# A four-layer gated cross-attention and experts block: layer 0's expert weights kept, attention in parts of TensorE's array, layer 3 as one pipeline

## The chip, the core and the metric

The kernel runs on one core of a Trainium2 chip. Five engines of the core work side by side, each with its own list of instructions in order: TensorE (PE: matmuls, transposes, and loads of its stationary operand, shown as PEld), VectorE (DVE), ScalarE (ACT), GpSimd (POOL) and SyncE (SP, which here only starts DMA transfers). They meet through semaphores. Matmul results land in PSUM, everything else lives in SBUF (128 partitions) or in device memory.

The metric is the device time of one execution in microseconds, the median of several runs. Everything is float32; in the profile one such matmul appears as two instructions, one transpose as one.

## The reference

`x` is 2 × 1024 tokens of width 256, the context 2 × 64 tokens. Four layers follow each other; each adds a gated attention on the context and then a gated feed-forward part, both on a normalised `x`:

```python
x = x + tanh(g_xattn[l]) * attention_l(layernorm(x), ctx)
x = x + tanh(g_ffn[l]) * ffn_l(layernorm(x))
```

What differs is the kind. With 16 heads of width 16 (layers 1 and 3):

```python
score = einsum('bhqd,bhkd->bhqk', qh, kh) / sqrt(16)
score = where(mask, score, -large)      # L1: a key mask; L3: a mask per query and key
out = einsum('bhqk,bhkd->bhqd', softmax(score), vh) @ Wo + bo
```

| layer | attention | feed-forward |
|---|---|---|
| 0 | linear, elu + 1 | each token to 1 of 8 experts (256 to 1024 to 256, relu), no capacity |
| 1 | 16 heads, softmax over 64 keys | sum of 8 dense experts, silu gate |
| 2 | one head | 1 of 8 experts, at most 384 tokens each, gelu |
| 3 | 16 heads, masked per query | 2 of 8 experts, at most 320 tokens each, relu, weights normalised over the two |

## The kernel before

The 2048 tokens are 16 tiles of 128, four tiles to a group of 512. The residual stream `xs` stays in SBUF as [128, 16, 256]. A scheduler may move instructions within each engine's list, so the order in the program is a starting point, not the final list.

**Layer 0's experts** (`moe0`, L973). The tokens are routed (a softmax over 8 logits, the largest), ranked within their expert by matmuls with triangular matrices, and sorted by expert into 23 tiles of at most 128 tokens (2048/128 + 8 − 1, so that any distribution fits). How many tiles an expert has is known on the chip only, so the loop over tiles is fixed and reads everything through indices: `rows_of` (L1031) is an indirect DMA with one row index for each partition. Per tile GpSimd issues six: two of 1 MB for the weights (`w`, L1032), two for the biases (`b1j`, `b2j`), one that gathers 128 normalised token rows (`xg`, in `gather_T`, L861), and a scatter that adds the result into the residual in device memory (`xd`, in `ffn`, L899). `ffn` (L879) multiplies with the first weight (`mm256`, L217: 8 blocks of output × 2 halves of the contraction), adds the bias and activates on ScalarE (L887), multiplies with the second weight (L892), and adds bias and token weight on VectorE (L897, L898). The weights rotate through the six buffers of `wpool`.

**Attention with 16 heads** (`Heads`, L343). Per group, `queries` (L419) forms qᵀ. Per tile, `scores` (L430) multiplies two blocks of 128 query rows (8 heads) with a block-diagonal matrix `kblk` of the keys, 512 columns each; VectorE adds a key bias (L1) or writes −large by a mask (L3, L446), takes the row maxima (L460) and subtracts them (L461); ScalarE takes one exponential of 1024 columns (L464). `values` (L467) transposes the probabilities in eight blocks, copies them to SBUF (L150), and multiplies each block, as the stationary operand, with `vaug`: 34 columns of values and ones, so that a sum for each head comes along (L486). VectorE takes 16 reciprocals per token (L494) and scales (L496). `output` (L499) transposes the result (L504), copies it, multiplies by `Wo`, and adds to the residual on VectorE (L512); GpSimd adds the output bias (L513). `group` (L515) staggers four tiles: scores of tile i, values of i − 1, output of i − 2.

In layer 1 the first group runs alone and the second likewise early; the others run among the dense experts (`middle`, L1323, whose products are L1210 and L1255 and keep TensorE occupied). In layer 3 `heads_xattn` (L529) first normalises all four groups (`normed`, L209) and then takes the groups in turn.

**Layers 2 and 3's experts** (`moe_capacity`, L1053). All tokens are normalised, `route` (L740) chooses for all 16 tiles at once and ranks them with 16 stages of matmul (L788, L790), `invert` (L803) turns the slots into a list of tokens per expert by comparing with a ramp (L818 to L829) and one matmul per tile (L831). Then for each of 8 experts the weights are loaded by SP, three gathers are issued by GpSimd, and `gather_T` and `ffn` follow. The next use of `xs` waits for `reload` (L855). After layer 2's experts, `heads3.setup` and layer 3's attention follow, then layer 3's routing and experts, then the copy to the output.

Of the kernel before, what the change touches and what calls it, by code (L numbers as in the profile page):

```python
# [8 lines left out]
F32 = mybir.dt.float32  # L9
# [25 lines left out]
L0_NTILE = N // L0_W + E - 1  # L35
L2_CAP = 384
# [5 lines left out]
def kernel(ctx: ExitStack, tc: tile.TileContext, a: dict, out: bass.AP):  # L42
# [37 lines left out]

    spare = int_ramp([P, 1], [[0, 1]], N, 1, "spare")
# [21 lines left out]
    halfmask = group_mask(SK, 2, "halfmask")  # L103
    sel16 = const.tile([P, HD], F32, name="sel16")
# [238 lines left out]
    class Heads:  # L343


        def __init__(self, pre, c_bk, r_bv, r_bo, gate, key_mask, full_mask):
# [3 lines left out]
            self.live = {}  # L350

        def setup(self, psp, tag):
# [10 lines left out]
            vaug = self.vaug = held.tile([P, B, H // 2, 2, HD + 1], F32, name="vaug")  # L363
# [37 lines left out]
            for b in range(B):  # L401
# [5 lines left out]
                    vaug[:, b, :, :, 0:HD],  # L407
# [3 lines left out]
                V.tensor_copy(  # L411
                    vaug[:, b, :, :, HD],
                    halfmask.unsqueeze(1).to_broadcast([P, H // 2, 2]),
                )
            self.tg = gates[:, self.gate : self.gate + 1]
            self.bo = held.tile([P, D], F32, name="bo")
            V.tensor_scalar_mul(self.bo, rows[:, self.r_bo, :], self.tg)

        def queries(self, g, hT, pools):  # L419
            two, py = pools["two"], pools["py"]  # L420
            qT = two.tile([P, NC, GW], F32, name="qT", bufs=1)
# [6 lines left out]
            self.qT = qT  # L428

        def scores(self, tt, pools):  # L430
# [3 lines left out]
            pr = two.tile([P, H, SK], F32, name="pr")  # L434
            HC = H // NC
            for c in range(NC):
                ps = pss.tile([P, 512], F32, name="ps_s")
                T.matmul(  # L438
                    ps,
                    lhsT=self.qT[:, c, t * P : (t + 1) * P],  # L440
                    rhs=self.kblk[:, b, c].rearrange("p j k -> p (j k)"),
                    start=True, stop=True,
                )
                ps3 = ps.rearrange("p (j k) -> p j k", k=SK)
# [6 lines left out]
                prc = pr[:, c * HC : (c + 1) * HC, :]  # L451
                if self.key_mask is not None:
                    V.tensor_add(
                        prc, ps3,
# [3 lines left out]
                    ps3 = prc  # L458
                mx = two.tile([P, HC], F32, name="mx")
                V.tensor_reduce(mx, ps3, AX.X, ALU.max)  # L460
                V.tensor_tensor(  # L461
                    prc, ps3, mx.unsqueeze(2).to_broadcast([P, HC, SK]), ALU.subtract
                )
            A.activation(pr, pr, AF.Exp)  # L464
            self.live[tt] = pr

        def values(self, tt, pools):  # L467

# [15 lines left out]
            w = 2 * (HD + 1)  # L484
# [14 lines left out]
        def output(self, tt, pools):  # L499
# [3 lines left out]
            for c in range(NC):  # L503
                T.transpose(  # L504
                    pst[:, c * P : (c + 1) * P], of[:, c * P : (c + 1) * P], ident
                )
# [992 lines left out]
```

## Time and profile before

| | us |
|---|---|
| three runs | 2445.48, 2451.8, 2453.09 |
| their median | 2451.8 |
| the profiled execution, its own time | 2437.11 |
| its span in the trace | 2435.4 |

The profiled execution is somewhat shorter than the three runs. Its mean granted TensorE clock was 0.929 of full speed. The page shows where the work lies; this is its first part, the busy time of each engine, its share of the span and the instructions, and three rows of its second part, in which the span is cut into 40 slices of 61 us and each digit is tenths of a slice:

```profile
PE 2189.6 (90%) x10132; PEld 1782.7 (73%) x10132; DVE 1210.5 (50%) x2695; ACT 797.9 (33%) x1523; POOL 1054.2 (43%) x1189
...
PE   5668887899999999999999999999968996886997
...
PEclk9759998999999999999999999999958998895998
DMA  3138886012222122222122222222323443010442
```

Slices 4 to 7 are layer 0's experts (the DMA row is highest there); the long run of nines is the dense experts of layer 1 with layer 2's attention; the last third of the row has layer 2's experts, layer 3's attention, its routing (a low digit of the clock), and its experts. A high busy digit at a low clock digit is no full engine: the same work takes longer there.

### The profile page before, as it was taken

To read this page: it belongs to the slowest core of one execution; us is meant where nothing else is said; L and a number is where in the kernel's file an instruction comes from. 1 tells how busy PE (TensorE), PEld (TensorE's weight loads), DVE (VectorE), ACT (ScalarE), POOL (GpSimd) and SP (SyncE) were. 2 spreads that over 40 slices of the span, in tenths; PEclk is the share of its full clock that TensorE was granted. 3 is DMA by queue.
4 is the path that set the end of the run, shared out by engine and by line. 5 is a ranking of instruction groups with operands and counts; after the bars stand their busy time and mean duration, and the time that the engine had idled before them with its cause. 6 is when DMAs were issued, how large, how long until landed. Compare 5 with 4: busy or idle time off the path is not lost.

```text
span 2435.4 us, 27851 instructions
## 1 busy us (share of the span) xinstructions
PE 2189.6 (90%) x10132; PEld 1782.7 (73%) x10132; DVE 1210.5 (50%) x2695; ACT 797.9 (33%) x1523; POOL 1054.2 (43%) x1189
## 2 busy tenths in 40 slices
PE   5668887899999999999999999999968996886997
PEld 3457776588888778887788887888856774565775
DVE  5631113675565766655855656566551116663111
ACT  5313331343333533334433334333311222230221
POOL 4116664136666346665366664666402320000331
PEclk9759998999999999999999999999958998895998
DMA  3138886012222122222122222222323443010442
GB/s 98 43 110 245 249 257 223 0 55 88 92 86 88 44 70 87 87 87 74 55 91 91 87 89 77 89 87 87 130 79 86 130 122 95 18 51 30 117 117 51
DMA packets 97545, 235.08 MB, mean 97 GB/s; under 512 B 13184, under 2 KB 41088, under 8 KB 86976
## 3 DMA queue, kind: packets, MB, share of 16 engines
q1 hardware_dynamic: 70880, 159.14, 20.3%
q0 software_dynamic: 21456, 68.92, 10.3%
q10 hardware_dynamic: 5072, 5.23, 0.6%
q8 instruction: 81, 1.33, 0.2%
q14 instruction: 56, 0.46, 0.1%
HBM read 211.10 MB, written 24.25 MB: 97 GB/s over the span
## 4 chain that ended last, share of the span: by engine, by line
PE 76%; DVE 10%; DMA 4%; POOL 2%; ACT 2%; issue 2%; POOLq 0%; DVEq 0%; ACTq 0%; SPq 0%
PE ps_b L1210 13%; PE ps_m L217 11%; PE ps_e L1210 9%; PE ps_a L1210 9%; PE ps_y L892 8%; PE ps_b L1255 6%; PE ps_a L1255 4%; PE ps_e L1255 4%; PE ps_y L486 2%; PE ps_y L217 2%; DMA xg<-hd,idx 1%; DVE st L159 1%; PE ps_tr L205 1%; DMA xd_L<-y_ff,idx 1%; PE ps_y L438 1%
## 5 line engine op out<-in xcount | busy, mean ns | idle before, releaser
L1210 PE MATMUL ps_b<-xsum,w 128*128 128x256 f32 x1536 | 388.2, 381 | 2.3 <-DVE c L1236 2.2
L1210 PEld LDWEIGHTS ps_b<-xsum,w 128*128 128x128 f32 x1536 | 289.7, 190 | 47.6 <-issue 4.6
L1117 POOL TENSOR_TENSOR w<-w 128x256 f32<-128x256 f32 x192 | 141.3, 736 | 400.5 <-DMA w<-in_L_Wu_dram 176.8
L217 PE MATMUL ps_m<-xT,w 128*128 128x128 f32 (+2 forms) x1248 | 260.6, 372 | 16.4 <-DVE xT L152 16.0
L1210 PE MATMUL ps_a<-hT,w 128*128 128x256 f32 x1024 | 270.1, 384 | 0.6 <-DVE hT L152 0.6
L892 PE MATMUL ps_y<-w,mid 128*128 128x256 f32 (+1 forms) x1136 | 254.0, 380 | 1.0 <-ACT mid L887 0.6
L217 PEld LDWEIGHTS ps_m<-xT,w 128*128 128x128 f32 x1248 | 195.6, 208 | 76.1 <-DVE xT L152 23.2
L892 PEld LDWEIGHTS ps_y<-w,mid 128*128 128x128 f32 (+1 forms) x1136 | 206.2, 184 | 41.5 <-issue 3.4
L1162 ACT COPY u<-ps_b 128x512 f32<-128x512 f32 (+1 forms) x192 | 98.8, 514 | 410.9 <-PE ps_b L1255 263.6
L1210 PEld LDWEIGHTS ps_a<-hT,w 128*128 128x128 f32 x1024 | 194.3, 192 | 30.3 <-issue 3.2
L899 POOL DMA_INDIRECT xd_L<-y_ff,idx x48 | 75.1, 1566 | 231.7 <-DVE y_ff L898 133.4
L897 DVE TENSOR_TENSOR y_ff<-ps_y,b 128x256 f32<-128x256 f32 (+1 forms) x48 | 20.3, 423 | 297.1 <-PE ps_y L892 297.1
L1118 POOL TENSOR_TENSOR w<-w 128x256 f32<-128x256 f32 x192 | 167.8, 874 | 0.0
L1119 POOL TENSOR_TENSOR w<-w 128x256 f32<-128x256 f32 x192 | 165.7, 863 | 0.0
L1120 POOL TENSOR_TENSOR w<-w 128x256 f32<-128x256 f32 x192 | 158.9, 827 | 14.7
L1210 PE MATMUL ps_e<-hT,w 128*128 128x256 f32 x512 | 134.8, 384 | 0.0
L1255 PE MATMUL ps_b<-t,w 128*128 128x256 f32 x512 | 133.2, 384 | 0.9 <-DVE accT L1273 0.9
L1210 PE MATMUL ps_e<-xsum,w 128*128 128x256 f32 x512 | 133.7, 382 | 0.0
L1255 PE MATMUL ps_a<-b,w 128*128 128x256 f32 x512 | 132.0, 379 | 0.0
L1144 ACT COPY ps_b<-ps_a 128x512 f32<-128x512 f32 (+1 forms) x192 | 96.1, 501 | 109.0 <-DVE b L1240 63.0
L1272 POOL TENSOR_TENSOR m<-m,accT 128x256 f32<-128x256 f32 x60 | 71.7, 1195 | 123.9 <-ACT m L1150 121.9
L150 ACT COPY xT<-ps_tr 128x128 f32<-128x128 f32 (+2 forms) x39 | 13.4, 343 | 327.8 <-PE ps_tr L875 257.1
(351 smaller groups left out, 3871.1 us busy)
## 6 DMA issues: line engine op xcount, KB each, us to landing
w<-in_L_Wg_dram SPq DMA_DIRECT2D x64, 512.0 KB, 4.1
w<-in_L_Wu_dram SPq DMA_DIRECT2D x64, 512.0 KB, 4.1
w<-in_L_Wd_dram SPq DMA_DIRECT2D x64, 512.0 KB, 3.7
w<-in_L_W_dram SPq DMA_DIRECT2D x32, 1024.0 KB, 5.1
xd_L<-xs SPq DMA_DIRECT2D x8, 512.0 KB, 3.2
hd_L<-h SPq DMA_DIRECT2D x8, 512.0 KB, 3.0
xs<-in_x_dram SPq DMA_DIRECT2D x4, 512.0 KB
xd<-xs SPq DMA_DIRECT2D x4, 512.0 KB, 3.7
```

Source lines behind the costliest of these rows:

```text
L217: T.matmul(ps, lhsT=lhs(c), rhs=rhs(c), start=(c == 0), stop=(c == n - 1))
L892: T.matmul(ps[:w, :], lhsT=mid[:, f, at : at + w], rhs=w2[:, f, :], start=(f == 0), stop=(f == NF - 1),)
L899: G.indirect_dma_start(out=xd[:, :], out_offset=bass.IndirectOffsetOnAxis(ap=idx[:w, j0 + s : j0 + s + 1], axis=0), in_=y[:w, :], in_offse ...
L1117: G.tensor_add(s[0], a21, a22)
L1118: G.tensor_sub(s[1], s[0], a11)
L1119: G.tensor_sub(s[2], a11, a21)
L1120: G.tensor_sub(s[3], a12, s[1])
L1144: A.copy(self.b, self.pa)
L1162: A.copy(u2, self.b)
L1210: T.matmul(ps[:, q * 256 : (q + 1) * 256], lhsT=lhs[kind][:, q, :], rhs=xr[kind], start=(first and q == 0), stop=True, skip_group_check=True,)
L1255: T.matmul(ps, lhsT=wd[kind][:, q, :], rhs=m["rhs"][kind][:, q * 256 : (q + 1) * 256], start=(clear and q == 0), stop=True, skip_group_che ...
L1272: G.tensor_add(sb, sb, acc[:, i, j])
```

## The change

Five things change; the code below is the core of the diff.

1. *Layer 0's tiles run as three interleaved streams* that start at tiles 0, 8 and 16. Each stream has two weight buffers and two bias tiles of its own. `again` marks tiles whose expert is that of the tile before in the stream; for these the indices of all partitions but the first are moved out of bounds by 4096 rows, and the fetch, which now has a bounds check, leaves these rows out. Fetches and the gather of tokens of a tile are issued three tiles ahead. `gather_T` is split into `gather` and `turn`.

```diff
+            V.tensor_tensor(again[:, 1:], ex[:, 1:], ex[:, : L0_NTILE - 1], ALU.is_equal)
...
+            V.tensor_scalar(again, again, beyond, None, ALU.mult)
...
+            V.tensor_scalar(wrow, ex, partid, None, ALU.add)
-            for j in range(L0_NTILE):
-                w1 = view1(rows_of(wpool.tile([P, 2048], F32, name="w"), "L0_W1", wrow, j))
...
-                gather_T(xgp, xT, pt, hd, idx, j, [L0_W])
...
+            def fetch(s, j):
+                w1, w2, b1, b2 = kept[s]
+                for dst, name, index, last in (
+                    (w1, "L0_W1", wrow, E * P - 1), (b1, "L0_b1", wrow, E * P - 1),
+                    (w2, "L0_W2", wrow, E * P - 1), (b2, "L0_b2", ex_i, E - 1),
+                ):
+                    G.indirect_dma_start(
+                        out=dst, out_offset=None, in_=a[name],
+                        in_offset=bass.IndirectOffsetOnAxis(ap=index[:, j : j + 1], axis=0),
+                        bounds_check=last, oob_is_err=False,
+                    )
+                return gather(xgp, hd, idx, j, [L0_W])
+            ahead = [fetch(*order[i]) for i in range(3)]
+            for i, (s, j) in enumerate(order):
...
+                turn(xT, pt, ahead.pop(0), [L0_W])
+                ffn(
...
+                if i + 3 < L0_NTILE:
+                    ahead.append(fetch(*order[i + 3]))
```

2. *Scores in halves of the array's rows.* Each product with 128 rows is two products with 64 rows and 256 columns, and the two halves go to different PSUM tiles. In layer 3 the maxima come negated and serve as bias of 16 exponentials of 64 columns each; the subtraction on VectorE goes.

```diff
+            pair = [pss.tile([P, 512], F32, name="ps_s") for _ in range(2)]
             for c in range(NC):
...
+                for r in range(2):
+                    T.matmul(
+                        pair[r][:, c * 256 : (c + 1) * 256],
+                        lhsT=self.qT[tt // TG][r * 64 : (r + 1) * 64, c, t * P : (t + 1) * P],
+                        rhs=self.kblk[r * 64 : (r + 1) * 64, b, c, r * 4 : (r + 1) * 4]
+                        .rearrange("p j k -> p (j k)"),
...
+                    V.tensor_reduce(mx, ps3, AX.X, ALU.max, negate=True)
+                    for j in range(HC):
+                        c, k = divmod(j, HC // NC)
+                        A.activation(
+                            prv[:, r, c, k], ps3[:, j], AF.Exp, bias=mx[:, j : j + 1]
+                        )
```

3. *Values in strips of 32 columns.* The stationary operand is now a block of 32 columns, of ones (`halves`) or of values (`vblk`), and the moving one the transposed probabilities; the result comes out transposed, and the sums come 16 times each. The two transposes of the output and their copy go. In layer 1 two reciprocals of 128 columns are taken; in layer 3 a logarithm and an exponential on ScalarE and three operations on VectorE, one of which corrects the reciprocal (the sign goes into the gate `less`). The output bias is added once for each group in `queries`.

```diff
-                T.matmul(
-                    pso[:, hp * w : (hp + 1) * w],
-                    lhsT=pT[:, hp, :],
-                    rhs=self.vaug[:, b, hp].rearrange("p a d -> p (a d)"),
...
+            for at, den in ((D, True), (0, False)):
+                for c in range(NC):
+                    for i in range(4):
+                        w = halves if den else self.vblk[:, b, c * 4 + i]
+                        T.matmul(
+                            pso[i * 32 : (i + 1) * 32, at + c * P : at + (c + 1) * P],
+                            lhsT=w.rearrange("p a d -> p (a d)"),
+                            rhs=pT[:, c * 4 + i, :],
+                            start=True, stop=True, skip_group_check=True,
+                        )
...
+            if pools.get("by_log"):
...
+                A.activation(rs, pso[:, D:], AF.Ln)
+                A.activation(rs, rs, AF.Exp, scale=-1.0)
+                V.tensor_mul(of, pso[:, :D], rs)
+                V.tensor_mul(rs, pso[:, D:], rs)
+                V.scalar_tensor_tensor(of, rs, 2.0, of, ALU.subtract, ALU.mult)
+            else:
+                for c in range(NC):
+                    cs = slice(c * P, (c + 1) * P)
+                    V.reciprocal(rs[:, cs], pso[:, D + c * P : D + (c + 1) * P])
+                V.tensor_mul(of, pso[:, :D], rs)
```

4. *Layer 3's attention as one pipeline over 16 tiles*, with its routing by groups. `ready` normalises a group (on ScalarE) and forms its queries; `onward` normalises the finished group for the experts and hands it to `Router.group`, which chooses (`choose`, already in use for layer 0), inverts the group's four tiles and adds the result to `sums`. The instruction that loads ScalarE's table for exponential and logarithm is placed behind layer 2's last activation. `heads_xattn` goes; `route` and `invert` remain for layer 2.

```diff
+            with tc.issue_after(done[0].ins):
+                A.preload_act_table_set("natural_log_exp_and_others")
+            router3.open()
...
+            ready(0)
+            for i in range(NT + 2):
+                if i < NT:
+                    heads3.scores(i, pools)
+                if 0 <= i - 1 < NT:
+                    heads3.values(i - 1, pools)
+                if i % TG == 1 and i + TG - 1 < NT:
+                    ready(i // TG + 1)
+                if 0 <= i - 2:
+                    heads3.output(i - 2, pools)
+                if i > TG and i % TG == 1:
+                    onward(i // TG - 1)
```

```diff
+        def group(self, g, h, hT, psp, rp):
...
+            picks = choose(psp, rp, g, hT, self.which, self.bias, self.top, self.before)
...
+            for i, (p1, _, ex, rk) in enumerate(picks):
...
+                for t in range(TG):
+                    T.matmul(
+                        pi[:, : 2 * NSLOT], lhsT=ohl[:, t, :],
+                        rhs=ohh[:, t].rearrange("p a j -> p (a j)"),
+                        start=(i == 0 and t == 0), stop=(i == self.top - 1 and t == TG - 1),
+                    )
+            V.tensor_add(
+                self.sums, pi[:, : 2 * NSLOT].rearrange("p (a j) -> p a j", a=2), self.sums
+            )
```

5. *Layers 2 and 3's experts* name the weights and gathers of the next expert before the work of the present one.

```diff
+            ahead = fetch(0)
             for e in range(E):
...
+                w1, w2, got = ahead
+                if e + 1 < E:
+                    ahead = fetch(e + 1)
...
+                turn(xT, pt, got, widths)
```

## The prediction

> **What bounds the kernel now.** I read first the page's busy shares (TensorE 90%), then a table of busy time by stretch, and in each stretch that is not full the chain of waits and the groups of instructions. In the table, the columns are the stretch, its length, the busy time (and instructions) of TensorE's matmuls, its weight loads, VectorE, ScalarE and GpSimd; then granted clock, DMA share and GB/s.
>
> ```profile
> 164.00:405.00 241.00, 201.59 (x1198) 178.79 (x1199) 26.16 (x82) 73.34 (x207) 146.51 (x138) 0.91 0.78 245
> 405.00:466.00 61.00, 45.69 (x215) 29.39 (x214) 41.96 (x125) 12.56 (x20) 20.81 (x29) 0.86 0.27 89
> 466.00:1790.00 1324.00, 1298.82 (x6024) 1102.54 (x6023) 841.57 (x1505) 518.96 (x942) 721.48 (x876) 0.99 0.26 82
> ...
> 2036.00:2190.00 154.00, 128.33 (x609) 86.43 (x610) 111.54 (x321) 49.06 (x77) 10.97 (x15) 0.88 0.11 39
> 2190.00:2252.00 62.00, 38.15 (x201) 36.20 (x200) 24.18 (x88) 3.08 (x6) 6.21 (x7) 0.56 0.12 41
> ```
>
> Four stages follow. Layer 0's experts (164 to 405) move 245 GB/s at a DMA share of 0.78. The middle (466 to 1790) is full on TensorE: only 25 us of 1324 idle. Layer 3's attention (2036 to 2190) has TensorE at 128 of 154 us, but at clock 0.88, where records are stretched; VectorE has 112. Its routing (2190 to 2252) fills no engine: a chain of latencies. The experts of layers 2 and 3 are full streams of matmuls.
>
> **Layer 0's weights.** The chain of waits, start and length in us, for one tile:
>
> ```profile
> 263.82 5.47 PE ps_m L217 x32
> 269.28 3.47 PE ps_y L892 x16
> ...
> 273.87 4.12 DMA xd<-y_ff,idx
> 278.33 0.95 POOL b2j L1032
> 279.58 3.88 DMA xg<-hd,idx
> ...
> 284.29 5.46 PE ps_m L217 x32
> ```
>
> One tile takes 284.29 − 263.82 = 20.5 us when it waits for its gathered tokens (`xg`) and these wait in the DMA queue and behind GpSimd's issues; another takes 8 to 10. From the first transpose (175.9) to the end of the last output (402.7) are 227 us for 23 tiles, 9.87 each. The change keeps weights (fetches with 127 of 128 rows out of bounds when the expert repeats) and issues gathers and fetches three tiles ahead. The first three tiles still need their full 6 MB, as now. Afterwards the new floor of a tile is on TensorE: transposes 0.45 and the copy of the result 0.3 (both at 283.5 in this chain), first product 3.84 (this row's length at full clock, at 205 us; 5.46 is the reduced clock), second 3.47, some gaps: 8.2 us. On GpSimd it is the issues, from its timeline (last column: idle before):
>
> ```profile
> 205.64 1.62 POOL L899 DMA_INDIRECT xd<-y_ff,idx  x1 [2.58 <-DVE y_ff L898]
> 207.56 0.98 POOL L1032 DMA_INDIRECT b1j<-in_L_b_dram,wrow  x1 [0.30 <-issue]
> ```
>
> The scatter 1.62 + 0.3 and five others at 0.95 + 0.3 make 8.2 us too: removing the transfers leaves the issues. I take 8.4 us × 23 = 193: **−33 us**. The unknown is what an issue costs that checks bounds; no row shows one. Below, it may cost less than 0.95 (a gather of 64 rows took 0.28 at 2247.6), but then TensorE's 8.2 binds: −38. Above, the dearest issue shown is the scatter's 1.62: 8.2 + 4 × 0.67 = 10.9 per tile, +24. I take 0.95, the same indices being read. The five added VectorE operations ahead of the first fetch are 0.2 us each; 1 us, inside the 0.4.
>
> **Attention in parts of the array, layer 1.** Per tile of 128 tokens at full clock TensorE now spends 4 × 0.43 on scores, 8 × 0.11 on transposes, 16 × 0.11 on values, 0.25 on transposing the output, 4 × 0.216 on the output product. New: scores are eight instructions of 256 columns on half arrays, values 32 of 128 columns on 32-column strips, the output transposes vanish. A row shows row halves already (layer 2's values), in TensorE's timeline:
>
> ```profile
> 874.97 0.59 PE L1255 MATMUL ps_e<-b,w 128*128 128x256 f32 x2
> 875.49 0.61 PE L644 MATMUL ps_y<-pT,vh 64*16 64x256 f32 x4
> 876.03 0.48 PE L1255 MATMUL ps_e<-b,w 128*128 128x256 f32 x1
> ```
>
> From start to start, four half-array instructions take 0.54 us, against about 0.43 for two full ones: the halves run together, and changing over costs at most 0.11. The Trainium skill ("TensorEngine Tiling (Array Packing)", Key Properties) speaks against the change in one point, that a change of tiling mode drains TensorE, and for it in another, that separate tiles work in parallel. Priced from the row, drains are 4 changes × 0.11 = 0.44 per tile; scores then cost 0.87 instead of 1.73. For strips of columns no row exists. Serial they cost 32 × 0.108 = 3.46 per tile; by the page's "up to 4×" for 32 columns, 0.87. The half-array row is nearest and confirms the independence, so I take 0.87, against 1.87 now. TensorE: −0.86 − 1.0 − 0.25 + 0.5 = −1.6 per tile; only the 12 tiles beside full TensorE count: −19.
>
> VectorE gets dearer: denominators come replicated, so 16 reciprocals per partition become 256.
>
> ```profile
> L494 DVE RECIPROCAL rs<-ps_y x32: 244/258/259, 440.7 to 2185.3; 128x16 f32<-128x16 f32 x32
> ...
> L628 DVE RECIPROCAL rs<-sm x4: 169/178/179, 872.6 to 1782.6; 128x4 f32<-128x4 f32 x4
> ```
>
> The slope is (258 − 178)/12 = 6.6 ns per element: 128 columns are 0.15 + 0.85 = 1.0 us, twice per tile. The skill ("VectorE: DVE Perf Modes", First, the fixed hardware budget) gives a reciprocal a repeat count of 8; at the page's clock of 0.96 GHz that is 8.3 ns, an estimate of 1.2 us. The rows decide: +1.75 per tile (+2.1 by the page). In the first groups (405 to 466, VectorE 42 of 61 us, latencies all) this is on the path: +1.75 × 4, less the removed transposes, copy and GpSimd's add of the bias (0.79 per tile): +3. In the middle VectorE has 480 us to spare, but each tile's chain is longer, and TensorE's order is fixed: +4 of stalls. Sum of layer 1: **−11** (ends −25, without stalls and with half of VectorE's part hidden, and +19 with serial strips: 12 × (3.46 − 0.87) = 31 more, so −19 + 31 + 3 + 4).
>
> **Layer 3's attention and routing.** Per tile VectorE loses two subtractions (0.67 each), a reciprocal; it gains three 256-column operations for one (0.41 to 0.48). Normalising goes to ScalarE, and the exponential becomes 16 of 64 columns: about 0.21 start to start, from the line through 0.368 us at 128 and 0.527 at 320 columns: 3.4 per tile, with 2 copies of 0.49, logarithm and exponential 0.7: ScalarE 5 us × 16 + norms ≈ 97. VectorE's list up to the last output: masks 23.5, maxima 21.6, statistics 20, three operations × 16 ≈ 20, residuals 7.7, routing of three groups: some 117 us in all (103 to 132, dependent operations being 0.1 apart more). TensorE at full clock needs 16 × (0.87 + 0.87 + 0.87 + 0.87 + 0.44) = 63, and queries and norms' transposes 17. So VectorE bounds. A head of 14 us (statistics, normalise, transpose, queries, first scores) precedes, and I add a few us for waits between engines: 136 us from the reload at 2036.6, the last output at 2172.6 against 2190.2. Layer 2's last weights hide the table load for exponentials; uncovered it would be a us or two.
>
> Then the routing, which now stands between last output and first expert:
>
> ```profile
> 2199.65 5.98 PE ps_m L217 x32
> ...
> 2212.83 6.21 PE ps_m L790 x30
> ...
> 2226.20 7.07 PE ps_m L831 x32
> ...
> 2237.38 7.07 PE ps_m L831 x32
> ```
>
> Together 26 of 62 us are matmuls over all 16 tiles at a clock of 0.56; two 2.2 us comparisons over 16 tiles each also go. By groups only the last quarter remains late: norm 9, choice and inversion 17 (layer 0's one-choice version runs about 11 from 149 us), gathers 7.5: 34. First expert at 2207 instead of 2252: **−45** (ends −20 if VectorE's routing of earlier groups, 75 small operations or 15 to 19 us each, delays the attention; −60 if only ScalarE's 97 bounds).
>
> **Experts of layers 2 and 3:** the fetch one expert ahead names the next weights (SP's queue) and gathers (GpSimd's) before the previous expert's product and scatters. GpSimd's timeline has that already: at 2294.7 and 2300.9 the next expert's gathers stand between the scatters of 2292.4, 2299.1 and 2308.8, and TensorE is full there: 0.
>
> **Sum.** −33 − 11 − 45 = −89. The profiled execution took 2437.1 (span 2435.4), 14.7 below the median of the runs, 2451.8: 2348 in its own measure, **2362** against the median.
>
> **Rivals.** *Strips run one after another* (0.15): for it, no row shows strips, and every short matmul is bound by loading weights (0.11 for 34 columns). Values 3.46 per tile, layer 3's TensorE 63 + 41 + 17 = 121 plus drains and waits, so its body saves nothing and only 25 of the routing stay; layer 1 +19: −33 − 25 + 19 = −39, about 2413. *Layer 3's pipeline fills poorly* (0.2): routing of earlier groups sits in VectorE's order before the next masks; layer 3 gives −20: 2387. For it, VectorE is the nearest to full; against it, 62 us of latency chains are known to shrink. *Skipping does not skip* (0.1): rows still move, 2 MB per tile at 250 to 290 GB/s is 7.2 to 8.4 us; layer 0 still about −28, since the gathers come early: 2367. *The bounds check is dear* (0.05, the slower side): GpSimd's cycle is 8.2 + 4δ; layer 0's gain is gone at δ = 0.42, the whole's at (89 + 5)/92 ≈ 1.0, an issue of 1.95 us. At 2.3 us it is 13.6 per tile, layer 0 +86 and the whole about −56 + 86 = +30: 2482. Against: no indirect row exceeds 1.62.
>
> **Numbers.** Forecast 0.5, rivals as given. The range runs from 2315 (all lower ends, −38 − 25 − 60 = −123, are 2329, less the 14 by which executions of one kernel differ here) to 2414 (strips serial); that leaves out the dear check and little else. What a measurement of this kernel can tell from no change is about 0.3%, 7 us: faster 0.94, same 0.01, slower 0.05.
>
> **What would show it.** Layer 0: DMA share from 0.78 to about 0.4, clock near 1.00, no waits of L875 for `xg`, a period of 8.4, issues with a check at 0.95. Strips: 32 matmuls starting within 0.9 us, or 3.5. Reciprocals of 128 columns at 1.0 us. Layer 3: last output near 2172 (less what comes off before), 34 us to the first expert, VectorE nearly full between. The forecast falls altogether if the checked issues pass 1.9 us.

## The result: 0.7% faster where 3.6% was forecast

The changed kernel took 2426.8 us (median of five runs, 2422.8 to 2434.5) beside 2445.5 us for the kernel before (2438.8 to 2453.1): ratio 0.9929, interval 0.9901 to 0.9957. The forecast was 2362, within 2315 to 2414; the measured time lies above that range. (Before's 2445.5 is the median of five runs of this measurement, the three of the table ahead among them.) Unmodified and measured five times, the same program had a median near 2426 twice and near 2399 three times, and the difference lies almost wholly in layer 0; so kernels are compared only with what was measured beside them.

The profiled execution took 2434.5 (span 2432.8), before 2437.1 (span 2435.4): in the two traces only 2.6 us lie between the kernels, less than the medians show. The table of busy time by stretch, with the columns used for the kernel before (length; TensorE's matmuls, weight loads, VectorE, ScalarE, GpSimd; clock, DMA share, GB/s), for the changed kernel:

```profile
178.00:402.00 224.00, 189.08 (x1161) 170.51 (x1162) 22.91 (x71) 73.00 (x207) 143.14 (x130) 0.94 0.44 123
402.00:466.00 64.00, 46.35 (x294) 28.76 (x293) 47.12 (x135) 11.07 (x16) 20.59 (x26) 0.80 0.25 85
466.00:1780.00 1314.00, 1283.17 (x6230) 1085.48 (x6229) 860.82 (x1518) 513.59 (x928) 715.83 (x867) 0.99 0.27 83
...
2030.00:2184.00 154.00, 132.22 (x880) 84.71 (x880) 96.38 (x332) 101.63 (x359) 9.49 (x4) 0.78 0.12 41
2184.00:2249.00 65.00, 41.40 (x249) 32.94 (x250) 26.32 (x154) 13.68 (x39) 5.85 (x7) 0.58 0.10 34
```

and from its page the busy shares, the clock and DMA rows of the 40 slices, and the queue of GpSimd's transfers:

```profile
PE 2181.9 (90%) x10740; PEld 1762.1 (72%) x10740; DVE 1220.6 (50%) x2795; ACT 855.5 (35%) x1820; POOL 1050.7 (43%) x1165
...
PEclk9759998899999999999999999999958996875998
DMA  3124516012223122222222222222413542010442
...
q0 software_dynamic: 21456, 40.15, 7.1%
```

The reader is to see three things. In layer 0 a good part of the transfers is gone (DMA share 0.78 to 0.44; the queue's 68.92 MB became 40.15), and the stretch is hardly shorter. In layer 3 (2030 on) the attention's clock is 0.78 where it was 0.88, so TensorE's 132 busy us are partly the same work stretched, and the attention runs on to 2214.5, beyond the row that ends at 2184. The dense stretch is shorter by some us.

Stages by marks that all these traces have: first transpose of layer 0, its last product, first dense product, start of the last product into `ps_a` (some 18 us of dense work follow it in every trace and count to the next stage), issue of layer 3's reload, last attention output, first transposes for an expert of layer 3. "Again" is the changed kernel in the third measurement; the last column, `l3_pipe_all`, is the best kernel of the experiments:

| stage, us | before | after | again | l3_pipe_all |
|---|---|---|---|---|
| layer 0's tiles | 226.8 | 222.5 | 198.6 | 196.1 |
| to the first dense product | 63.0 | 63.9 | 66.3 | 65.3 |
| dense products | 1280.9 | 1273.8 | 1267.8 | 1272.8 |
| to layer 2's experts, and these | 285.8 | 287.7 | 287.6 | 287.1 |
| layer 3: reload to last output | 157.8 | 188.3 | 185.0 | 127.3 |
| last output to first expert | 57.8 | 29.9 | 29.8 | 58.3 |
| what remains | 187.4 | 188.4 | 188.8 | 188.9 |
| span | 2435.4 | 2432.8 | 2401.7 | 2373.7 |

The start up to layer 0 is 175.9, 178.3, 177.7 and 177.8. Two terms fail: layer 0 (−4.3 for −33) in the measurement of record, and layer 3 (+2.6 for −45) in every one: in the five traces of this kernel its two stages together differ by −1.5 to +2.6 from before.

### The profile page after: what moved, and what is told of

Its sections match the earlier page's. It is cut to its first block, busy times and chain, and to the rows that moved or that the text cites. A ratio compares the mean times of both kernels' runs of the same rounds, so it can differ in the third digit from the quotient of the medians.

```text
span 2432.8 us, 29532 instructions
## 1 busy us (share of the span) xinstructions
PE 2181.9 (90%) x10740; PEld 1762.1 (72%) x10740; DVE 1220.6 (50%) x2795; ACT 855.5 (35%) x1820; POOL 1050.7 (43%) x1165
## 3 DMA queue, kind: packets, MB, share of 16 engines
q0 software_dynamic: 21456, 40.15, 7.1%
## 5 line engine op out<-in xcount | busy, mean ns | idle before, releaser
L922 DVE TENSOR_TENSOR y_ff<-ps_y,b 128x256 f32<-128x256 f32 (+1 forms) x71 | 30.1, 424 | 499.3 <-PE ps_y L917 421.3
L912 ACT ACTIVATE mid<-ps_m,b 128x128 f32<-128x128 f32 (+2 forms) x312 | 137.8, 444 | 168.7 <-PE ps_m L224 150.8
L1374 DVE TENSOR_TENSOR b<-b,c 128x512 f32<-128x512 f32 x128 | 116.4, 910 | 4.0
```

What stands on the lines that cost most here:

```text
L912: done[0] = A.activation(mid[:, f, :n], ps[:, :n], func, bias=b1[:, f : f + 1])
L1374: V.tensor_mul(m[name], m[name], c)
```

## Experiments

Theories. Layer 3: (1) the routing of earlier groups stands as a block in the in-order lists and each group costs its whole chain; (2) the pipeline's new instructions (strips, 64-column exponentials, logarithm) are slow in themselves. Layer 0: (1) skipping works and something else sets the rhythm; (2) the checked fetches or the streams cost what the transfers saved. All kernels below are the changed kernel with one edit (`l3_pipe_all_turn` has two); "beside" means in the same measurement.

### Second measurement: parts undone

`l0_old` takes layer 0 from the kernel before.

```diff
-            ahead = [fetch(*order[i]) for i in range(3)]
-            for i, (s, j) in enumerate(order):
+            for j in range(L0_NTILE):
+                w1 = view1(rows_of(wpool.tile([P, 2048], F32, name="w"), "L0_W1", wrow, j))
```

> The changed kernel with layer 0's experts as before (rotating weight buffers, every row fetched, tokens gathered per tile). Theory 1, the trace's: keeping the weights gave layer 0 almost nothing (214 us from first transpose to last in the changed kernel, 219 before), so this is within 5 us of the changed kernel, about 2430. Rival, the prediction's: keeping them is worth 33 us, and something else in the changed kernel lost it again; then this is about 2460.

`l3_old` takes layer 3's order from the kernel before: all groups normalised, group after group, then routing of all 16 tiles at once. With the order come back the old numbers of buffers and the normalising on VectorE. The new instructions (halves, strips, 64-column exponentials, the logarithm) stay.

```diff
-    last_attention()
-    xd = moe_capacity("L3", L3_CAP, router3.close, AF.Relu)
+    heads_xattn(heads3)
+    xd = moe_capacity("L3", L3_CAP, route_all3, AF.Relu)
```

> The changed kernel with layer 3 in the old order: all groups normalised first, group after group, routing over all 16 tiles at the end; attention in parts of the array, the 16 exponentials and the logarithm stay. Theory 1: the pipeline pays 30 us of attention for 28 us of routing, so this is within 5 us of the changed kernel, about 2427, with the last output near 2185 and 62 us from there to the first expert. Rival: the attention is slow because of its new instructions (64-column exponentials, strips), not because of the pipeline and its routing; then the last output stays near 2214 and the time is 2450 to 2460.

`l0_turn` puts the next tile's transposes (`between`) between a tile's two products and holds the second product (`held_back`) until they are issued.

```diff
+        if between is not None:
+            last = between()
...
+                held_back = tc.issue_after(last.ins)
...
+            with held_back:
```

> The changed kernel with one edit: in layer 0 the transposes of the next tile stand between the first and the second product of the present tile, so that TensorE has no gap of 0.5 to 3 us between tiles. Theory 1: the tile's 9.7 us instead of 8.4 come from TensorE running slowly after such gaps; without them the period is GpSimd's 8.5 us, layer 0 is 20 to 28 us shorter, about 2403. Rival: the slow stretches come from the indirect DMAs and GpSimd's issues beside the products; then the period stays at 9.3 to 9.7 and the time within 10 us of the changed kernel.

`l3_late` keeps the pipeline and the routing by groups, but all four groups are routed after it.

```diff
-                if i > TG and i % TG == 1:
-                    onward(i // TG - 1)
+            for g in range(NG):
+                onward(g)
```

> The changed kernel with the routing of all four groups behind the pipeline instead of between its tiles. Theory 1: routing between the tiles is what makes the attention 30 us longer (every engine's list is in order); then the last output moves from 2214 to about 2180 and the three further groups of routing, pipelined behind each other, cost 30 to 40: the time stays within 8 us. Rival: the attention is slow by itself, TensorE at half clock and waiting; then the last output stays after 2205 and the time is 20 to 35 us longer, about 2455.

Measured beside before at 2441.3:

| | median | ratio (interval) | layer 0 | reload to last output | to first expert |
|---|---|---|---|---|---|
| l0_old | 2424.0 | 0.9927 (0.9902–0.9951) | 227.3 | 188.1 | 29.9 |
| l3_old | 2410.3 | 0.9868 (0.9823–0.9913) | 195.8 | 167.5 | 56.0 |
| l0_turn | 2406.0 | 0.9850 (0.9807–0.9893) | 200.6 | 183.7 | 29.8 |
| l3_late | 2399.0 | 0.9829 (0.9788–0.9870) | 196.3 | 136.9 | 78.8 |

Layer 0: with the change 196, without it 227 in the same measurement. The layer-0 part is worth 31 us here, where the trace of record gives 4. `l0_old` came out at 2424.0, near the 2430 of theory 1 as it was expected, but for another reason: the kernels beside it, which keep the change in layer 0, were quick there. So its theory 1, that keeping the weights gives almost nothing, falls. Where `l0_turn` comes near what was expected of it, that is for another reason: the layer was already quick in this measurement, and the edit makes it 4 us slower than its neighbours (200.6 against 196).

Layer 3: moving the routing out of the pipeline shortens the body from 184–188 to 136.9, (185 − 137)/3 = 16 us for each of three groups. But all four chains then stand one after another, 78.8 us, some 20 each, so the sum stays. `l3_old` with the same instructions in the old order takes 223.5 in both parts, more than the 215.6 of before: the instructions in the old order bring nothing, though buffers and normalising went back with it and how much of the 8 us is theirs is not separated.

### Third measurement: the two ways tried at once

`after_again` is the changed kernel as it is.

> The changed kernel once more, not a letter different. Layer 0 has run in two ways with the same instructions: 222 us in the changed kernel, 196 in the two kernels that differ from it in layer 3 alone. Theory 1: which one is settled by small shifts of time that belong to a program; then layer 0 takes 222 us again and the time is about 2426. Rival: it is a matter of the chip or the hour; then layer 0 takes 196 here and the time is about 2400.

`l0_fill` puts four products of the identity with itself, whose result is overwritten, between a tile's transposes and its first product, to keep TensorE occupied there.

```diff
+            with tc.issue_after(turned.ins):
+                for _ in range(FILL):
+                    fill = T.matmul(spare_ps[:, :P], lhsT=ident, rhs=ident, start=True, stop=True)
+            behind = tc.issue_after(fill.ins)
```

> The changed kernel with four idle products (identity by identity, overwritten by the real result) in layer 0 between a tile's transposes and its first product, where TensorE waits for the copy of the tokens. Theory 1: the slow stretches of layer 0 follow from the clock that drops after such gaps; with the gaps filled the clock stays at full, the period is 8.4 to 8.7 us and layer 0 takes 196 to 203: about 2403. Rival: the stretches come from elsewhere (DMA traffic, the semaphores of the indirect DMAs); then they stay and each tile costs some tenths more, 2427 to 2440.

`l3_pipe_all` keeps the pipeline over 16 tiles and puts the routing of the kernel before, over all 16 tiles at once, behind it.

```diff
-                if i > TG and i % TG == 1:
-                    onward(i // TG - 1)
...
-    xd = moe_capacity("L3", L3_CAP, router3.close, AF.Relu)
+    xd = moe_capacity("L3", L3_CAP, route_all3, AF.Relu)
```

> The changed kernel with the pipeline over 16 tiles, but layer 3's routing over all 16 tiles at once behind it, as before. Theory 1: the routing between the tiles takes its whole chain of waits out of the attention; without it the last output comes 137 us after the reload (188 in the changed kernel), and the old routing costs 56 from there: 25 us less in this stage, 2375 where layer 0 runs in 196 us and 2401 where it takes 222. Rival: the pipeline is slow with its own instructions; then 188 + 56 and 2450.

`l3_pipe_all_turn` adds the edit of `l0_turn` to it.

> Both: the pipeline with the old routing behind it, and layer 0's next transposes between the two products of a tile. Theory 1: layer 0 at 196 to 200 us and layer 3's stage at 193: 2375 to 2380, faster than both kernels. Rival: the sum does not hold because a gain moves the clock elsewhere; 2395 or more.

Beside before at 2437.9: `after_again` 2399.6 (0.9834, 0.9780–0.9888), `l0_fill` 2396.8 (0.9824, 0.9771–0.9877), `l3_pipe_all` **2371.2** (0.9715, 0.9661–0.9768), `l3_pipe_all_turn` 2377.5 (0.9744, 0.9691–0.9796). The table by stretch, first of `after_again`, then of `l3_pipe_all`, then of `l3_late`; layer 3 is the attention up to the last output, then up to the first expert:

```profile
178.00:376.00 198.00, 178.42 (x1150) 161.84 (x1149) 21.79 (x67) 73.65 (x207) 142.86 (x129) 0.97 0.49 138
1998.00:2183.10 185.10, 154.57 (x1064) 102.52 (x1064) 110.84 (x414) 110.67 (x387) 9.49 (x4) 0.77 0.12 41
2183.10:2212.90 29.80, 13.20 (x57) 11.81 (x57) 11.38 (x72) 3.79 (x9) 2.38 (x3) 0.50 0.12 40
```

```profile
178.00:374.00 196.00, 176.42 (x1153) 159.35 (x1153) 21.61 (x68) 73.64 (x207) 142.86 (x129) 0.98 0.49 139
1999.20:2126.40 127.20, 109.72 (x913) 69.20 (x914) 93.05 (x259) 99.10 (x361) 9.39 (x4) 0.90 0.16 54
2126.40:2184.80 58.40, 35.47 (x179) 34.78 (x178) 22.52 (x86) 2.07 (x4) 2.40 (x3) 0.53 0.09 33
```

```profile
1993.70:2130.50 136.80, 118.26 (x930) 75.17 (x930) 86.09 (x228) 106.29 (x381) 9.38 (x4) 0.85 0.15 51
2130.50:2209.30 78.80, 42.91 (x193) 39.79 (x190) 37.50 (x258) 6.47 (x16) 2.29 (x3) 0.53 0.07 22
```

With the routing inside, VectorE is busy for 110.8 of 185.1 us: its added work is 18 us against `l3_pipe_all` and 25 against `l3_late` (110.8 − 86.1), and the time added is 58 and 48. No engine is full: TensorE is the busiest, 154.6 of 185.1, but at a clock of 0.77 instead of 0.90. The body waits. Without the routing it takes 127.3, 127.3, 130.3 and 130.4 in the four traces of this pipeline, some 10 us less than the 137 expected of this run after `l3_late`, and the old routing behind it costs no more than before (58). What makes the 10 us between `l3_late` and `l3_pipe_all` was not looked into. Theory 1 stands for layer 3, theory 2 falls.

One part is not separated. In the changed kernel TensorE's granted clock is 0.50 while it waits for the routing (2096.3 to 2113.4, 2140.7 to 2157.8 and 2178.3 to 2191.9); in the body of `l3_pipe_all`, behind its head, only from 2020.6 to 2027.4 and for 3 us at 2116. The matmuls of the chain that is waited for run at this low clock too, and no run tells its share from that of the order.

### Fourth measurement: the order inside the pipeline, and layer 1

`after_third` is the changed kernel again.

> The changed kernel a third time, unchanged: 2426.8 in its first measurement, 2399.6 in its second, all of the difference in layer 0 (222 us and 198). Theory 1: layer 0 has two rhythms, and what sets it is outside the program; then one of the two times comes again, 2400 or 2427, with layer 0 at 196 to 199 or at 222. Rival: the times lie anywhere between; then a third value of layer 0, around 205 to 215.

`l1_old` gives layer 1 the attention of the kernel before (class `Heads` as it was); layer 3 keeps the new one.

```diff
-    heads1 = Heads("L1", C_BK1, R_BV1, R_BO1, 1, a["key_mask"], None)
+    heads1 = HeadsOld("L1", C_BK1, R_BV1, R_BO1, 1, a["key_mask"], None)
```

> The changed kernel with layer 1's attention as before (whole array, 16 reciprocals, output transposed on TensorE); layer 3's stays in parts. Theory 1: the parts are worth what the prediction said, 11 us in layer 1, seen between the first dense product and the last (1281 us before, 1268 to 1274 in the changed kernel); then this stretch is 8 to 14 us longer than in the changed kernel measured beside it and the stretch ahead of it some 1 to 3 us shorter. Rival: the parts do nothing there and the difference is scatter; then both stretches are within 2 us.

`l3_lag` issues each group's routing two tiles later.

```diff
-                if i > TG and i % TG == 1:
-                    onward(i // TG - 1)
+                if i > TG + 2 and (i - 2) % TG == 1:
+                    onward((i - 2) // TG - 1)
+            onward(NG - 1)
```

> The changed kernel with each group's routing named two tiles later in the pipeline (the last two groups' close to its end). Theory 1: each group's routing costs its whole chain, 17 us, because it stands as a block in the engines' lists ahead of the next tiles' masks and maxima; two tiles later the masks of two tiles stand between its steps for the first two groups, and the stage from the reload to the first expert takes 195 to 207 instead of 215. Rival: routing costs 17 us for each group wherever it stands, since engines are lacking and not order; then 213 to 218.

Beside before at 2442.2: `after_third` 2425.3 (0.9923, 0.9894–0.9952), `l1_old` 2441.4 (0.9991, 0.9977–1.0005), `l3_lag` 2416.0 (0.9885, 0.9846–0.9924). Layer 0 was at 222 to 224 in all three. Layer 3 up to the first expert: 214.1 with the changed order, 197.2 two tiles later, so the place alone is worth 17 us. What it does is seen in VectorE's timeline (start, length; in brackets idle time before and what ended it). The changed kernel:

```profile
2101.42 0.16 DVE L196 SCALAR_TENSOR_TENSOR off<-mv,rstd 128x4 f32<-128x4 f32 x1
2108.18 0.19 DVE L703 TENSOR_TENSOR r_pr<-ps_m,e_bias 128x32 f32<-128x32 f32 x1 [6.60 <-PE ps_m L224]
...
2109.88 0.19 DVE L708 TENSOR_REDUCE r_m<-r_pr 128x4 f32<-128x32 f32 x1 [1.06 <-ACT r_pr L707]
...
2120.86 0.75 DVE L461 COPY_PREDICATED_SCALAR ps_s<-dropm,negs 128x512 f32 x1
```

`l3_lag`:

```profile
2085.24 0.26 DVE L196 SCALAR_TENSOR_TENSOR off<-mv,rstd 128x4 f32<-128x4 f32 x2
...
2094.89 0.19 DVE L703 TENSOR_TENSOR r_pr<-ps_m,e_bias 128x32 f32<-128x32 f32 x1 [0.63 <-PE ps_m L224]
...
2095.65 0.18 DVE L705 TENSOR_REDUCE r_m<-r_pr 128x4 f32<-128x32 f32 x1
2096.12 0.75 DVE L461 COPY_PREDICATED_SCALAR ps_s<-dropm,negs 128x512 f32 x1 [0.29 <-PE ps_s L450]
2096.78 0.18 DVE L706 TENSOR_TENSOR r_pr<-r_pr,r_m 128x32 f32<-128x32 f32 x1
2096.88 1.28 DVE L475 TENSOR_REDUCE mx<-ps_s 128x8 f32<-128x512 f32 x2
```

In the first, VectorE stands still for 6.6 us until the router's logits come (they need normalise, transposes, copies and 16 short products first), and the next tile's mask, L461, is 19.4 us behind the last operation of the norm. In the second, the logits come 9.7 us after the norm's last operation, even later than the 6.8 us above, but VectorE has attention work meanwhile and waits 0.63 us; and masks and maxima stand between the routing's operations. So what the chain costs depends on what stands beside it in the list. Some 34 us over a body without routing remain (161.6 − 127.3).

For layer 1, `l1_old` has a dense stretch of 1279.6 against 1275.0, and 67.6 against 65.0 ahead of it. That is 7.2 us; the medians lie 16.1 apart, of which 3.7 are layer 3's stage in the profiled executions, where the program is the same. Both stretches miss what was expected (8 to 14 of the dense one, and 1 to 3 us in favour of the old attention ahead of it). The sign is clear: in all 18 traces with the new attention in layer 1 the dense stretch is 1267.8 to 1275.0, in the two with the old 1279.6 and 1280.9. The size is known no better than 7 to 16.

### Fifth and sixth measurements

The same kernels once more, to meet layer 0's slow rhythm beside the two edits that fill its gap, and to confirm the best kernel.

> The changed kernel, unchanged, as the measure for the two kernels beside it. It has shown layer 0 at 222 to 224 us (2425 to 2427) in two measurements and at 198.6 (2399.6) in one; one of the two is expected again.

> The kernel with four idle products in layer 0's gaps, again. If the changed kernel beside it takes 222 to 224 us in layer 0: theory 1, that the slow rhythm is kept up by gaps of TensorE, has this kernel at 196 to 203; the rival, that TensorE is slowed there by something that gaps do not cause, has it at 215 or more. If the changed kernel takes 196 to 199, this takes the same and nothing is told.

> The kernel with layer 0's next transposes between the two products, again; it removes the gap in another way. If the changed kernel beside it takes 222 to 224 us in layer 0: theory 1 has this at 196 to 204, the rival at 215 or more.

> The pipeline with the old routing behind it, again: 2371 where layer 0 took 196 us. If layer 0 takes 222 here, theory 1 expects the same gain in layer 3's stage (185 to 190 us against 214 in the changed kernel) and a time of about 2397; a stage of 200 or more would mean that the gain belonged to that measurement.

Beside before at 2439.6: `after_fourth` 2399.7 (0.9844, 0.9813–0.9876), `l0_fill_2` 2400.0 (0.9848, 0.9814–0.9882), `l0_turn_2` 2408.6 (0.9877, 0.9843–0.9912), `l3_pipe_all_2` 2370.3 (0.9718, 0.9689–0.9747).

> The changed kernel, unchanged, as the measure for the two beside it: layer 0 at 222 to 224 us or at 196 to 199.

> Four idle products in layer 0's gaps, a third time, for a measurement in which the changed kernel beside it has the slow layer 0. Theory 1 (gaps keep the slow rhythm up): 196 to 203 us; rival (something that gaps do not cause): 215 or more. If the changed kernel takes 196 to 199, nothing is told.

> The pipeline with the old routing behind it, a third time, for the same measurement: layer 3's stage at 185 to 190 us whatever layer 0 does; about 2370 with the fast layer 0 and 2397 with the slow one.

Beside before at 2435.6: `after_fifth` 2398.4 (0.9846, 0.9813–0.9878), `l0_fill_3` 2405.9 (0.9877, 0.9831–0.9922), `l3_pipe_all_3` 2371.0 (0.9733, 0.9702–0.9765). The slow rhythm did not come again, so whether either edit cures it is open. Where it is absent, `l0_fill` brings nothing (and was 7.5 us slower once) and `l0_turn` costs 6 to 9 us. `l3_pipe_all` was 2370 to 2371 three times, 28 us below the changed kernel beside it each time (28.3, 29.4, 27.4): the version to keep.

## Why the forecast was wrong, step by step

**Layer 0, −33.** The step's mechanism is right. GpSimd's timeline in the changed kernel:

```profile
241.46 1.04 POOL L1083 DMA_INDIRECT w<-in_L_W_dram,wrow  x1 [0.31 <-PE ps_m L224]
242.81 1.01 POOL L1083 DMA_INDIRECT b<-in_L_b_dram,wrow  x1 [0.30 <-issue]
...
248.01 1.62 POOL L924 DMA_INDIRECT xd<-y_ff,idx  x1 [0.30 <-issue]
```

A checked issue (one with the bounds check) takes 0.99 to 1.04, once 1.26, where 0.95 was taken; a round of six, from one scatter's start to the next, takes 8.5 (239.54 to 248.01), forecast 8.2. TensorE waits for gathered tokens once, 5.6 us at the start, and never again. In three of five measurements of this kernel, layer 0 takes 195.7 to 198.6 (195.7 is `after_fourth`), 29 to 32 less than `l0_old`'s 227.3: the −33 was nearly paid. In the measurement of record and in the fourth it was not, though the program is the same. There the tiles come in a pattern of 8.4, 8.6 and 12.1 us. TensorE's timeline from the tile ahead of a long one into the long one:

```profile
247.45 4.41 PE L224 MATMUL ps_m<-xT,w 128*128 128x128 f32 x32 [0.89 <-DVE y_ff L923]
251.70 3.62 PE L917 MATMUL ps_y<-w,mid 128*128 128x256 f32 x16
255.16 0.38 PE L898 MATMUL ps_tr<-ident,xg 128*128 128x128 f32 x2
258.51 5.47 PE L224 MATMUL ps_m<-xT,w 128*128 128x128 f32 x32 [2.97 <-DVE xT L159]
```

and ScalarE's at the same time, the activations that read the first of these products:

```profile
249.96 0.37 ACT L912 ACTIVATE mid<-ps_m,b 128x128 f32<-128x128 f32 x1 [0.95 <-PE ps_m L224]
250.73 0.37 ACT L912 ACTIVATE mid<-ps_m,b 128x128 f32<-128x128 f32 x1 [0.40 <-PE ps_m L224]
251.47 0.37 ACT L912 ACTIVATE mid<-ps_m,b 128x128 f32<-128x128 f32 x1 [0.37 <-PE ps_m L224]
```

In `after_again` TensorE has

```profile
246.06 3.84 PE L224 MATMUL ps_m<-xT,w 128*128 128x128 f32 x32 [0.89 <-DVE xT L159]
249.74 3.62 PE L917 MATMUL ps_y<-w,mid 128*128 128x256 f32 x16
253.20 0.38 PE L898 MATMUL ps_tr<-ident,xg 128*128 128x128 f32 x2
```

and eight activations in one row of 3.49 us, 0.45 from start to start. In the trace of record they come some 0.75 apart, each waiting for TensorE: the results come late, although the recorded starts look nearly regular (32 of them in 4.41 us for 3.84). The clock is not what makes them late: it was 1.00 from 247.45 to 251.86. The copy of the output then starts at 257.4, some 2 us after the recorded end of the second product, the next tile's transposes are copied behind it, TensorE stands still for 2.97 us, and its next first product runs at a mean clock of 0.69, 5.47 instead of 3.84. The Trainium skill ("TensorE: Matmul & The Clock Gate", Part 1) has the reduced clock follow at least one idle window of about 3.4 us; here it followed 2.97 us, so the measured wait decides and is shorter than the page's figure. That explains what follows the late results, not why they are late.

Three things narrow it. DMA packets are as long in both cases (median 309 ns for 8 KB). No gap between tiles starts it: in the very first tile two activations are already 2.11 us apart (184.77 and 186.88; 2.82 in `after_third`), where in the traces of the quick rhythm no two are more than 0.86 apart there. And the kernel before has late results too, in the trace of record, in ScalarE's timeline

```profile
328.97 0.37 ACT L887 ACTIVATE mid<-ps_m,b1j 128x128 f32<-128x128 f32 x1 [1.26 <-PE ps_m L217]
331.13 0.37 ACT L887 ACTIVATE mid<-ps_m,b1j 128x128 f32<-128x128 f32 x1 [1.79 <-PE ps_y L892]
```

and in 10 of its 23 tiles, where they cost nothing: its layer 0 took 226.8 us, and the same layer without late results, in `l0_old`, 227.3. The old layer waits for its tokens anyway; the new one has no slack left, so the delay shows. The lateness thus goes with the measurement (every execution of a kernel in it, and all three changed kernels of the fourth), not with the change; nor with the chip, since the sixth measurement ran on the chip of the fourth and was quick. **What starts the slow rhythm stays open.** The step that failed is the floor of 8.2 us for a tile, which takes TensorE's results as there when its records end and leaves nothing for their delay; the rest of the step stands, and which rhythm the measurement of record would meet was bad luck.

Two readings of the forecast are to be set right, though its sum does not rest on them: the 20.5 us from 263.82 to 284.29 span two tiles (a first product stands at 273.84 between them), and the gather of 64 rows took 0.92 at 2247.6, 0.28 being its part of the chain of waits.

**Layer 1, −11.** The dense stretch lost 7.1 us in the trace of record and 4.6 beside `l1_old`. Strips run side by side, as taken; TensorE's timeline of layer 3 shows them plainest:

```profile
2085.01 1.13 PE L450 MATMUL ps_s<-kblk,qT 64*128 64x256 f32 x4 [0.30 <-ACT pr L478]
2086.07 0.43 PE L515 MATMUL ps_y<-pT,halves 128*32 128x128 f32 x8
2086.31 0.62 PE L515 MATMUL ps_y<-pT,vblk 128*32 128x128 f32 x16
2086.86 0.66 PE L212 MATMUL ps_tr<-ident,h 128*128 128x128 f32 x4
```

Sixteen and the change of mode behind them take 0.55 us from start to start; the four of a block start 7 ns apart, and a whole tile's 32 take 1.0 to 1.1 with the change of mode, for which 0.87 was taken and 3.46 feared. The reciprocal was priced twice; its row:

```profile
L535 DVE RECIPROCAL rs<-ps_y x32: 886/944/958, 438.9 to 1175.0; 128x128 f32<-128x128 f32 x32
```

It took 0.94 us, against 1.0 from the slope and 1.2 by the estimate from the repeat count of 8 in the Trainium skill ("VectorE: DVE Perf Modes", First, the fixed hardware budget); the measurement decides. The change of mode was taken at 0.11 and costs about 0.2 on leaving strips and 0.3 on entering (start to start, where 0.11 to 0.216 is usual).

The scores are the term that was off: the first row above has four half-array instructions and the change of mode behind them in 1.06 us, where 0.43 and 0.11 were counted. Mean distances of starts in layer 1 give an estimate: eight at 0.196 are 1.57 us per tile against 1.79 before, a saving of 0.2 where 0.86 was forecast; values and their ones 32 × 0.034 = 1.1 against 1.7, a saving of 0.6 where 1.0 was forecast. With the transposes saved and the changes of mode paid TensorE gains about 0.9 us per tile, not 1.6. So that the sum came near is partly luck: less was gained, and less was lost in stalls and in the first groups. The loss of 3 us in the first groups did not come: beside `l1_old`, the changed kernel is 2.6 quicker there. (The forecast's lower end of −25 does not follow from its terms: −19 and some 2 are −17.)

**Layer 3, −45: the step that failed.** The tail is right: last output at 2214.5, first product of an expert at 2248.5 in the chain of waits,

```profile
2214.47 0.50 DVE xs L546
...
2220.46 3.66 PE ps_m L224 x16
...
2236.37 3.66 PE ps_m L1177 x16
...
2245.17 2.39 DMA xg<-hd_L,r_idx
2247.56 0.45 issue
2248.01 0.45 PE ps_tr L898
2248.46 1.61 PE ps_m L224 x3
```

34.0 us, forecast 34. The body is wrong: 188.3 from the reload's issue, forecast 140 (136 from its arrival, some 4 later). The step that failed is "So VectorE bounds", with "I add a few us for waits between engines: 136 us". VectorE's busy time was summed rightly: 117 forecast, of which some 24 are the routing of three groups, and 110.8 measured in `after_again`. What was wrong is the time beside it: 23 forecast (14 of head, some 5 of waits, 4 for the reload), 74 measured (185.1 − 110.8). Without the routing it is 34 (127.2 − 93.1, in `l3_pipe_all`). So the routing adds 18 us of busy time and 40 of waiting. Its operations depend on each other across VectorE, TensorE and ScalarE, and in lists that run in order the attention of the next tiles stands behind each of them: each group cost 16 to 19 us, a third of the 48 and 58 above, where the sum had 8.

The pipeline without routing missed too: its forecast is 140 − 24 = 116, and it took 127 to 130 in `l3_pipe_all`, 137 in `l3_late`. These 11 to 21 us are other waits between engines, which no run takes apart.

The first part was at hand. The forecast's lower end reads "15 to 19 us each, delays the attention", which is what was measured; three groups at 15 to 19, less the 24 that were in the sum, are 21 to 33 us more, and the end of −20 follows from that. The rest of the way to +2.6 is the 11 to 21 us of other waits. The second rival, whose mechanism is the one that ran, was named and given 0.2, and under-priced by some 20 us for the same reason.

**Experts of layers 2 and 3, 0.** Right: the stage with layer 2's experts went from 190.3 to 192.0, the last stage from 187.4 to 188.4.

**The other rivals.** Strips one after another: not so. Skipping that does not skip: 40.15 MB, not so. A dear check: 1.04 us, not so.

## What to carry to other kernels

When work is interleaved into engines that run their lists in order, price it by the length of its chain at the place where it stands, and let busy time count only when the order shows other work between its links. Here the sum of the bounding engine's busy time was right to 6 us and the body 48 us off. Latency-bound work of several groups is best put into one wide chain behind the pipeline: one chain over 16 tiles took 58 us, four over four tiles 79 alone and 48 to 58 for only three inside the pipeline. Where the same program can fall into two rhythms, measure variants side by side and repeat the unmodified kernel in each measurement.

## What the runs showed of the hardware that was not expected

- Skipped rows still make packets. The queue of GpSimd's transfers has 21,456 packets before and after, with 68.92 and 40.15 MB; only the lengths differ.
- One program, two rhythms: layer 0 at 222.5 to 224.3 us in two measurements (in the fourth with all three kernels) and at 195.7 to 198.6 in three. In the slow one TensorE's results come late at a full granted clock (1.00 from 247.45 to 251.86), and they do so in the kernel before as well, at no cost. The readers' waits (here ScalarE's activations) show it; TensorE's rows show it only in part.
- Two products on different halves of the rows can run together, but seldom did: pairs whose starts lie 7 + 209 or 86 + 130 ns apart take as long as one full product, 0.216 us for two; most start 0.216 after each other, and the mean in layer 1 is 0.196. What decides was not tested.
